# A graph network's second relational layer: neighbour sums in seven half-size block products, and other banks for the root product

## The chip, the cores and the metric

The kernel is one program on one core of a Trainium2 chip. The metric is device time in microseconds, from start to end of one execution; a time without further words is the median of several executions. Everything is in 32-bit floats.

The engines: TensorE (PE in the profile, with its weight loads as PEld) multiplies and writes its sums into PSUM, eight banks of 128 partitions by 512 floats. VectorE (DVE) and ScalarE (ACT) read PSUM and write SBUF. GpSimd (POOL) works on SBUF alone. SyncE (SP) issues most of the transfers. Each engine executes its instructions in the order of the program.

## The reference, cut to what matters

A residual block of attention over a graph of 384 nodes comes first, then a residual block with a two-layer relational graph convolution (768 features, six relations, four basis matrices). The change concerns the latter. Cut down to it:

```python
x = relu(h_text @ w_in + b_in)                       # 384 x 768
for l in range(2):
    h_in = x
    W = einsum('rb,bio->rio', comp[l], basis[l])     # six relations from four bases
    h_all = einsum('ni,rio->rno', x, W)
    msg = h_all[edge_type, src] / counts[edge_type, dst]
    x = segment_sum(msg, dst) + x @ root[l] + conv_bias[l]
    x = relu(x) + h_in
    x = gamma[l] * (x - mean(x, 0)) * rsqrt(var(x, 0) + 1e-5) + beta[l]
h_final = x @ w_out + b_out
return layernorm(h_final) * ln_gamma + ln_beta
```

The kernel turns the gather and the segment sum into dense products. With `H_b = x @ basis_b` for the four bases b, and a 384 x 384 matrix `At_b` for each (edge counts, divided by the degree of the target, mixed over the relations by `comp`), the neighbour sum is the sum over b of `At_b` times `H_b`. It is a product with a contraction of 4 x 384 = 1536.

## The kernel before, in words

The graph's tables are built from the edges in the first half of the kernel, on DVE and POOL, beside the projections of the attention block on PE. At about 388 us (the first L846) the relational layers begin.

Activations lie transposed, as `XT`: features on the partitions, six chunks of 128 (`KC`), by 384 nodes. One layer consists of

- four blocks b, each computing `H[b] = x @ basis_b`, nodes on the partitions (L831 to L872). This product already uses seven half-size products in place of eight. The bank names there are pe, pf, pb, pc and pa, taken by `next_bank` (L70), which hands out the eight banks in a ring, the one longest not taken first. DVE and ACT move and add the results into H (L852 to L867); the last product of a block is left to the next one (`rest`). Between the products DVE mixes the matrices `At` (L326, from `go_between`), and in the first layer the degree counts are computed too: `share` takes a bank `ps_cnt` (L337), and L340 reads it.
- the root product `x @ root` (L880), six output chunks of 128 features, each in a bank `pr[o]`, six matmuls of 384 columns each. `kept` (L835) names the bank that `rest` still needs, so that root's six are taken from the other seven (L877).
- the neighbour sums (`add_neighbours`, L892 to L901), added into the same six banks: for each output chunk o twelve matmuls with a 128x128 piece of H as the weights and 384 columns of `At` moving. All chunks first get bases 0 and 1, then each in turn gets bases 2 and 3.
- the normalisation of chunk o, as soon as its sums are complete (L905 to L918): ACT rectifies with the bias into a buffer `u`, DVE adds the residual into `XN`, measures mean and variance over the 384 nodes (`bn_stats`, `bn_aggr`), adds epsilon, ACT takes the square root, DVE takes the reciprocal, makes scale and offset in three operations on one column, and scales the chunk.

`XN` becomes the next `XT`. After the second layer the output projection (L939) multiplies three tiles of 128 nodes by `w_out`. For the first tile it takes chunks 0 to 3 of `XT` for both halves of the output first, then chunks 4 and 5. DVE normalises the rows and two queues send them out (L943 to L954).

PE, POOL, SP and DVE run in the order of the source (L57), and ACT from L472 on. In the second layer nothing is scheduled in another order than it is written. Waits between engines are derived from what each instruction reads and writes. In tile pools, tiles of one tag share memory: `H` has four buffers, one for a block; `A` holds the tables from which `At` is mixed, and after the last mixing, the rows `rowsB` (L888); `hT` and `mask8` hold the sums of the basis weights (`weight_sums`, L782).

Of the kernel before, what the change touches and what calls it, by code (L numbers as in the profile page):

```python
# [10 lines left out]
F32 = mybir.dt.float32  # L11
# [3 lines left out]
AF = mybir.ActivationFunctionType  # L15
ALU = mybir.AluOpType

P = 128
N = 384
# [32 lines left out]
def gnn_kernel(ctx: ExitStack, tc: tile.TileContext, out, x, edges, chunks, cols, rows, small,  # L52
# [712 lines left out]
    with tc.tile_pool(name="conv", bufs=1) as cp:  # L765
# [60 lines left out]
        T = weight_sums(w)  # L826
        for l in range(L):

            H_ = []
            rest = lambda: None  # L830
            for b in range(B):  # L831
                H_.append(cp.tile([P, NT, DC], F32, tag="H", name="H", bufs=4))
                hs = [[H_[b][:, n, i * HC:(i + 1) * HC] for i in range(2)] for n in range(NT)]
                pe, pf, pb, pc, pa = [next_bank("ps_g")[:, :N] for _ in range(5)]
                kept = ring[-1]  # L835

                def times(ps, x, y, start=False):

                    for c in range(3):
                        nc.tensor.matmul(ps, x[:, c], y(c), start=start and c == 0, stop=(c == 2),  # L840
                                         skip_group_check=not start)

                for c in range(3):
                    for ps, n, i, o, first in ((pa, 0, 0, 0, True), (pe, 2, 0, 0, True), (pf, 2, 0, 1, True),
                                               (pb, 0, 1, 0, True), (pe, 2, 1, 0, False), (pf, 2, 1, 1, False)):
                        nc.tensor.matmul(ps, block(XT, n, i)[:, c], w[c][:, i, o * HC:(o + 1) * HC],  # L846
                                         start=(first and c == 0), stop=(c == 2 and (i == 1 or ps is pa)))
                    if c == 0:
                        rest()
                        T4 = last_sums(w, T[1])  # L850
                    go_between(l, b, c)
                nc.scalar.copy(hs[0][0], pa)  # L852
                nc.vector.tensor_tensor(hs[0][0], hs[0][0], pb, ALU.add)
                times(pc, S[:, 0], lambda c: T[0][:, c], True)
                nc.scalar.copy(hs[2][0], pe)
                nc.scalar.copy(hs[2][1], pf)
                nc.scalar.copy(hs[1][1], pc)
                times(pa, S[:, 1], lambda c: T[1][:, c])
                nc.scalar.copy(hs[0][1], pa)
                times(pc, S[:, 3], lambda c: w[c][:, 1, HC:])  # L860
                nc.vector.tensor_tensor(hs[0][1], hs[0][1], pc, ALU.add)  # L861
                times(pa, S[:, 2], lambda c: T[2][:, c])
                nc.vector.tensor_tensor(hs[1][1], hs[1][1], pa, ALU.add)

                def rest(pa=pa, X=XT, T4=T4, dst=hs[1][0]):
                    times(pa, block(X, 1, 1), lambda c: T4[:, c])
                    nc.scalar.copy(dst, pa)  # L867

                if b + 1 < B:
                    w = load_basis(l, b + 1)  # L870
                    T = weight_sums(w)
                go_between(l, b, 4)  # L872


            w = [wload(root[l, part], "w_c") for part in range(3)]
            XN = xtp.tile([P, KC, N], F32, tag="XT", name="XN")
            pr = [next_bank("ps_c", [i for i in range(8) if i != kept])[:, :N] for _ in range(KC)]  # L877
            for k in range(KC):
                for o in range(KC):
                    nc.tensor.matmul(pr[o], w[k // 2][:, k % 2, o * P:(o + 1) * P], XT[:, k, :], start=(k == 0), stop=False)  # L880
                if k == 0:
                    rest()
                go_between(l, B, k)
            if l + 1 < L:
                w = load_basis(l + 1, 0)
            else:

                rowsB = late.tile([P, 3, D], F32, tag="A", name="rowsB")  # L888
                for j, r in enumerate((R_BOUT, R_LNG, R_LNB)):
                    nc.scalar.dma_start(rowsB[:, j, :], rows[r:r + 1, :].to_broadcast([P, D]))  # L890

            def add_neighbours(o, bs):  # L892
                for b in bs:
                    for n in range(NT):
                        nc.tensor.matmul(pr[o], H_[b][:, n, o * P:(o + 1) * P], At[:, b, n, :],  # L895
                                         start=False, stop=(b == B - 1 and n == NT - 1))

            for o in range(KC):
                add_neighbours(o, (0, 1))
            for o in range(KC):  # L900
                add_neighbours(o, (2, 3))  # L901
                ps = pr[o]
                c = l * KC + o
                u = cp.tile([P, N], F32, tag="u", name="u", bufs=2)
                nc.scalar.activation(u, ps, AF.Relu, bias=cols_sb[:, CB + c:CB + c + 1])  # L905
                nc.vector.tensor_tensor(XN[:, o, :], u, XT[:, o, :], ALU.add)  # L906
                st = tiny.tile([P, 6], F32, tag="stb", name="stb")
                nc.vector.bn_stats(st, XN[:, o, :])
                mv = tiny.tile([P, 2], F32, tag="mvb", name="mvb")
                nc.vector.bn_aggr(mv, st)  # L910
                sc = tiny.tile([P, 3], F32, tag="sc", name="sc")
                nc.vector.tensor_scalar(sc[:, 0:1], mv[:, 1:2], BN_EPS, None, ALU.add)
                nc.scalar.activation(sc[:, 0:1], sc[:, 0:1], AF.Sqrt)
                nc.vector.reciprocal(sc[:, 0:1], sc[:, 0:1])
                nc.vector.tensor_tensor(sc[:, 1:2], sc[:, 0:1], cols_sb[:, GAM + c:GAM + c + 1], ALU.mult)
                nc.vector.tensor_tensor(sc[:, 2:3], mv[:, 0:1], sc[:, 1:2], ALU.mult)
                nc.vector.tensor_tensor(sc[:, 2:3], cols_sb[:, BET + c:BET + c + 1], sc[:, 2:3], ALU.subtract)
                nc.vector.tensor_scalar(XN[:, o, :], XN[:, o, :], sc[:, 1:2], sc[:, 2:3], ALU.mult, ALU.add)  # L918
                if o == 2 and l + 1 < L:
                    T = weight_sums(w)  # L920
# [7 lines left out]
        w = [wload(w_out[part], "w_out") for part in range(3)]  # L928
        for t in range(NT):
            hf = cp.tile([P, NT * DC], F32, tag="H", name="hf", bufs=4)[:, :D]  # L930
            last = t == NT - 1
            ps = [next_bank("ps_f") for _ in range(3 if last else 2)]

            parts = [(ps[0], 0, 512), (ps[1][:, :256], 512, 768), (ps[2][:, :256], 768, D)] if last else \
                [(ps[0], 0, 512), (ps[1], 512, D)]
            for ks in ((range(4), range(4, KC)) if t == 0 else (range(KC),)):
                for p, c0, c1 in parts:
                    for k in ks:
                        nc.tensor.matmul(p, XT[:, k, t * P:(t + 1) * P], w[k // 2][:, k % 2, c0:c1],  # L939
                                         start=(k == 0), stop=(k == KC - 1))  # L940
            st = tiny.tile([P, 4, 6], F32, tag="st", name="st")
            for p, c0, c1 in parts:
                nc.vector.tensor_tensor(hf[:, c0:c1], p, rowsB[:, 0, c0:c1], ALU.add)  # L943
                for c in range(c0, c1, 256):
                    nc.vector.bn_stats(st[:, c // 256, :], hf[:, c:c + 256])
            mv, sd = row_spread(st)

            parts = ((nc.sync, slice(0, 512)), (nc.scalar, slice(512, D)))
            for _, cs in parts:
                nc.vector.scalar_tensor_tensor(hf[:, cs], hf[:, cs], mv[:, 0:1], rowsB[:, 1, cs], ALU.subtract, ALU.mult)  # L950
            nc.vector.reciprocal(sd, sd)
            for queue, cs in parts:
                nc.vector.scalar_tensor_tensor(hf[:, cs], hf[:, cs], sd, x_sb[:, t, cs], ALU.mult, ALU.add)
                queue.dma_start(out[t * P:(t + 1) * P, cs], hf[:, cs])  # L954
# [62 lines left out]
```

## Time and profile before

| what | us |
|---|---|
| median of three runs | 746.15 (744.75 to 747.71) |
| the profiled execution: its time | 747.49 |
| its span | 745.7 |
| PE busy | 724.6 |
| DVE busy | 435.3 |
| ACT busy | 141.8 |
| second layer: root product from 641.29 to 660.64 | 19.35 |
| second layer: neighbour sums from 660.64 to 707.08 | 46.44 |
| in these 46.44 us: DVE busy | 12.79 |
| in these 46.44 us: ACT busy | 3.92 |
| from 707.08 to the end of the span | 38.62 |

Times in the profile are microseconds from the span's start. A line of the timeline gives start, length, engine, source line, operation, what is written from what, and in brackets how long the engine had been idle before and what released it. A matmul in 32-bit floats is one instruction of the source and two records in the trace, each with a weight load. Matmuls are pipelined, so the time from one start to the next, not the duration of one, is what PE spends.

### The profile page before, as it was taken

How to read it: one execution, taken by the hardware profiler on the slowest of the kernel's cores; microseconds unless marked ns; L12 is line 12 of the kernel's file. 1: busy time of each engine (PE TensorE's matmuls, PEld its weight loads, DVE VectorE, ACT ScalarE, POOL GpSimd, SP SyncE). 2: the span in 40 equal slices, each digit the busy share in tenths (PEclk: the TensorE clock that was granted, in tenths of full speed). 3: DMA queues.
4: the chain of work that ended last, by engine and by line, in shares of the span. 5: the costliest groups of instructions: out<-in, count | busy, mean ns of one | idle time of the engine just before them, and what ended most of it. 6: DMA issues, size and time to landing. Idle time of an engine off the chain costs nothing.

```text
span 745.7 us, 7797 instructions
## 1 busy us (share of the span) xinstructions
PE 724.6 (97%) x2820; PEld 471.6 (63%) x2820; DVE 435.3 (58%) x1161; ACT 141.8 (19%) x324; POOL 321.0 (43%) x242
## 2 busy tenths in 40 slices
PE   8999999999999999999899999899999999999995
PEld 7755589999964444446885555555555555555543
DVE  5878518878405499444524699980287766000655
ACT  3301021111102377410121130100022111000200
POOL 1355767778786787587774464210000000210000
PEclk9999999999999999999999999999999999999999
DMA  7797677644356322624428943321003312700001
GB/s 294 254 346 247 190 183 210 202 148 112 114 145 208 57 2 2 212 1 85 86 1 208 277 149 128 127 84 43 0 1 127 113 67 82 289 1 0 0 29 56
DMA packets 40532, 90.94 MB, mean 122 GB/s; under 512 B 19644, under 2 KB 27680, under 8 KB 36270
## 3 DMA queue, kind: packets, MB, share of 16 engines
q1 hardware_dynamic: 18478, 79.62, 30.4%
q0 software_dynamic: 21008, 8.42, 10.3%
q10 hardware_dynamic: 1008, 2.41, 0.8%
q8 instruction: 22, 0.36, 0.2%
q14 instruction: 16, 0.13, 0.0%
HBM read 79.27 MB, written 11.16 MB: 121 GB/s over the span
## 4 chain that ended last, share of the span: by engine, by line
PE 87%; DVE 10%; issue 1%; ACT 1%; DMA 0%; DVEq 0%; ACTq 0%
PE ps_c L895 12%; PE ps_g L846 12%; PE ps_q L395 11%; PE ps_g L840 9%; PE ps_k L377 7%; PE ps_c L880 6%; PE ps_v L525 6%; PE ps_y L616 5%; PE ps_f L939 4%; PE ps_v L377 4%; PE ps_s L564 3%; PE ps_x L377 3%; PE ps_o L609 2%; PE ps_pT L598 2%; DVE same L250 2%; DVE At L326 2%
## 5 line engine op out<-in xcount | busy, mean ns | idle before, releaser
L266 POOL DMA_INDIRECT atab<-count,at x99 | 159.2, 1608 | 55.8 <-DMA atab<-count,at 30.0
L261 POOL DMA_INDIRECT mtab<-m_val,at x99 | 102.3, 1034 | 58.5 <-issue 23.5
L895 PE MATMUL ps_c<-At,H 128*128 128x384 f32 x288 | 93.2, 486 | 0.0
L895 PEld LDWEIGHTS ps_c<-At,H 128*128 128x128 f32 x288 | 54.7, 190 | 38.2
L927 POOL TENSOR_TENSOR x_sb<-x_sb,rowsB 128x1024 f32<-128x1024 f32 x3 | 6.9, 2342 | 159.9 <-DMA rowsB<-in_rows 159.9
L326 DVE SCALAR_TENSOR_TENSOR At<-A,small_sb,At 128x1152 f32<-128x1152 f32 x40 | 62.9, 1635 | 0.0
L840 PE MATMUL ps_g<-T,S 128*128 128x384 f32 x144 | 49.1, 486 | 0.0
L846 PE MATMUL ps_g<-w_c,XT 128*128 128x384 f32 x144 | 48.0, 487 | 0.9 <-DVE H L861 0.9
L846 PE MATMUL ps_g<-w_c,XN 128*128 128x384 f32 x144 | 47.6, 486 | 0.0
L395 PE MATMUL ps_q<-hT,w_q 128*128 128x384 f32 (+1 forms) x160 | 43.4, 436 | 1.4 <-ACT hT L90 1.4
L525 PE MATMUL ps_v<-w_v,v 128*128 128x512 f32 x96 | 41.9, 594 | 0.0
L395 PE MATMUL ps_q<-q,w_q 128*128 128x384 f32 x128 | 41.4, 486 | 0.0
L846 PEld LDWEIGHTS ps_g<-w_c,XT 128*128 128x128 f32 x144 | 27.2, 190 | 20.1 <-DVE H L861 1.5
L846 PEld LDWEIGHTS ps_g<-w_c,XN 128*128 128x128 f32 x144 | 27.4, 190 | 19.1
L840 PEld LDWEIGHTS ps_g<-T,S 128*128 128x128 f32 x144 | 27.4, 190 | 19.1
L395 PEld LDWEIGHTS ps_q<-hT,w_q 128*128 128x128 f32 x160 | 30.2, 200 | 14.1 <-ACT hT L90 1.7
L906 DVE TENSOR_TENSOR XN<-u,XN 128x384 f32<-128x384 f32 x6 | 3.4, 558 | 56.3 <-ACT u L905 56.3
L395 PEld LDWEIGHTS ps_q<-q,w_q 128*128 128x128 f32 x128 | 24.3, 190 | 17.0
L616 PE MATMUL ps_y<-w_o,attT 128*128 128x512 f32 x80 | 35.0, 595 | 0.0
L377 PE MATMUL ps_k<-T,S 128*128 128x192 f32 x192 | 35.0, 326 | 0.0
L342 POOL TENSOR_TENSOR A<-A,rn 128x1152 f32<-128x1152 f32 x6 | 20.1, 3354 | 30.7 <-DVE rn L341 30.7
L577 DVE CUSTOM_DVE_ANT_0 s<-ps_s,mask 128x384 f32<-128x384 f32 x48 | 24.5, 548 | 14.3 <-PE ps_s L564 14.3
(212 smaller groups left out, 1184.2 us busy)
## 6 DMA issues: line engine op xcount, KB each, us to landing
w_c<-in_basis SPq DMA_DIRECT2D x24, 768.0 KB, 6.1
atab<-zero SPq DMA_DIRECT2D x12, 576.0 KB, 7.6
A<-atab POOLq DMA_DIRECT2D x10, 576.0 KB, 10.2
w_c<-in_root SPq DMA_DIRECT2D x6, 768.0 KB, 6.0
w_q<-in_wq SPq DMA_DIRECT2D x4, 1024.0 KB, 11.6
w_q<-in_wiq SPq DMA_DIRECT2D x4, 1024.0 KB, 12.6
w_k<-in_wk SPq DMA_DIRECT2D x4, 1024.0 KB, 5.7
w_k<-in_wik SPq DMA_DIRECT2D x4, 1024.0 KB, 6.2
```

The lines of the kernel that those rows point to most:

```text
L261: nc.gpsimd.indirect_dma_start(mtab[c // PER][:, :], bass.IndirectOffsetOnAxis(at[:, 0, c:c + 1], 0), m_val[:, c:c + 1], None)
L266: nc.gpsimd.indirect_dma_start(atab[0 if i < 18 - DEALT else i % 2][:, :], bass.IndirectOffsetOnAxis(at[:, 1, c:c + 1], 0), count[:, 1, c: ...
L326: nc.vector.scalar_tensor_tensor(At[:, b], A[:, r], w, At[:, b], ALU.mult, ALU.add)
L377: nc.tensor.matmul(ps, a[:, k, :], b[:, k, :], start=start and k == 0, stop=(k == 3), skip_group_check=not start)
L395: nc.tensor.matmul(ps[o][:, c], wt_[:, k, o * P:(o + 1) * P], src[:, k, c], start=(k == 0 and c.start == 0), stop=(k == KD - 1 and c.stop ...
L525: nc.tensor.matmul(ps, v[:, k, t * P:(t + 1) * P], w[k // 4][:, k % 4, :], start=(k == 0), stop=(k == KD - 1))
L616: nc.tensor.matmul(ps, attT[:, k, t * P:(t + 1) * P], w_o[half][k // 4][:, k % 4, :], start=(k == 0), stop=(k == KD - 1))
L840: nc.tensor.matmul(ps, x[:, c], y(c), start=start and c == 0, stop=(c == 2), skip_group_check=not start)
L846: nc.tensor.matmul(ps, block(XT, n, i)[:, c], w[c][:, i, o * HC:(o + 1) * HC], start=(first and c == 0), stop=(c == 2 and (i == 1 or ps is ...
L880: nc.tensor.matmul(pr[o], w[k // 2][:, k % 2, o * P:(o + 1) * P], XT[:, k, :], start=(k == 0), stop=False)
L895: nc.tensor.matmul(pr[o], H_[b][:, n, o * P:(o + 1) * P], At[:, b, n, :], start=False, stop=(b == B - 1 and n == NT - 1))
L939: nc.tensor.matmul(p, XT[:, k, t * P:(t + 1) * P], w[k // 2][:, k % 2, c0:c1], start=(k == 0), stop=(k == KC - 1))
```

## The change

It has three parts.

**The second layer's neighbour sums.** The product is cut in two along each of its dimensions: the output features in pairs of chunks (2p and 2p+1), the nodes in two halves of 192 columns, and the contraction (twelve pieces of 128, four bases by three node tiles) in two groups of six. For every pair seven products of six matmuls with 192 columns replace the eight that these halves would need; some operands are sums of blocks. The sums of `At` (T1 to T4) are made once, ahead of the loop; those of H (`feature_sums`, four a pair) a pair ahead. The results of a product serve several quarters of the output. So only the first products of the three pairs are added into root's banks; ACT then moves each `pr[o]` with its bias into `XN` (`begin`, no rectifier), and DVE adds the rest from two further banks, `pa` and `pc`, while these are still being accumulated (`take`). A rectifier pass on ACT (`rectify`) follows when a chunk is complete. The normalisation is split into `measure` and `normalise_layer`, with reads of the banks (and sums of H) between the two. T3 and one sum of H for each pair are written in place.

**Tiles.** The four H tiles become one; `u` is gone, and in the first layer ACT writes the rectified chunk into `XN`, to which DVE adds the residual in place. `rowsB` becomes the first part of a larger tile `room` in the same memory, whose rest, with `hT` and `mask8`, holds the sums. The output rows `hf` become three parts of one tile in the place of H.

**Root's banks.** In both layers root's six banks now leave out the last two of the ring when a block's banks are taken, `pc` and `pa`, where they left out `pa`.

The diff, cut to its core:

```diff
@@ for l in range(L), blocks of H
-            H_ = []
+            H_ = cp.tile([P, B, NT, DC], F32, tag="H", name="H")
...
-                kept = ring[-1]
+                kept = ring[-2:]
...
-            pr = [next_bank("ps_c", [i for i in range(8) if i != kept])[:, :N] for _ in range(KC)]
+            pr = [next_bank("ps_c", [i for i in range(8) if i not in kept])[:, :N] for _ in range(KC)]
...
-                rowsB = late.tile([P, 3, D], F32, tag="A", name="rowsB")
+                room = late.tile([P, R * NT * N], F32, tag="A", name="room")
+                rowsB = room[:, :3 * D].rearrange("p (j d) -> p j d", j=3)
...
+            def measure(o):
+                nc.vector.tensor_tensor(XN[:, o, :], XN[:, o, :], XT[:, o, :], ALU.add)
...
+                nc.scalar.activation(sc[:, 0:1], sc[:, 0:1], AF.Sqrt)
+                return o, mv, sc
+            def normalise_layer(o, mv, sc):
+                c = l * KC + o
                 nc.vector.reciprocal(sc[:, 0:1], sc[:, 0:1])
...
+            def begin(o, func=AF.Identity):
+                c = l * KC + o
+                nc.scalar.activation(XN[:, o, :], pr[o], func, bias=cols_sb[:, CB + c:CB + c + 1])
+            if l + 1 < L:
+                for o in range(KC):
+                    add_neighbours(o, (0, 1))
+                for o in range(KC):
+                    add_neighbours(o, (2, 3))
+                    begin(o, AF.Relu)
+                    normalise_layer(*measure(o))
+                    if o == 2:
+                        T = weight_sums(w)
+            else:
+                def h(o, i):
+                    return H_.rearrange("p b n d -> p (b n) d")[:, i * 6:i * 6 + 6, o * P:(o + 1) * P]
+                def q(i, j):
+                    return At.rearrange("p b n d -> p (b n) d")[:, i * 6:i * 6 + 6, j * HN:(j + 1) * HN]
+                def times(ps, x, y, start=False, stop=True):
+                    for c in range(6):
+                        nc.tensor.matmul(ps, x[:, c], y[:, c], start=start and c == 0, stop=stop and c == 5,
+                                         skip_group_check=True)
...
+                nc.vector.tensor_tensor(T1, q(0, 1), q(0, 0), ALU.subtract)
+                nc.vector.tensor_tensor(T2, q(1, 1), T1, ALU.subtract)
+                T3 = q(0, 1)
+                nc.vector.tensor_tensor(T3, q(1, 1), q(0, 1), ALU.subtract)
+                nc.vector.tensor_tensor(T4, q(1, 0), T2, ALU.subtract)
...
+                def feature_sums(p):
+                    s0, s1, s3 = spaces[p % 2 * 3:][:3]
+                    o0, o1 = 2 * p, 2 * p + 1
+                    S.append((s0, s1, h(o1, 0), s3))
+                    for dst, x, y, op in ((s0, h(o1, 0), h(o1, 1), ALU.add), (s1, s0, h(o0, 0), ALU.subtract),
+                                          (h(o1, 0), h(o0, 0), h(o1, 0), ALU.subtract),
+                                          (s3, h(o0, 1), s1, ALU.subtract)):
+                        nc.vector.tensor_tensor(dst, x, y, op)
+                        yield
...
+                def take(o, j, ps):
+                    dst = XN[:, o, j * HN:(j + 1) * HN]
+                    nc.vector.tensor_tensor(dst, dst, ps, ALU.add)
+                def rectify(o):
+                    nc.scalar.activation(XN[:, o, :], XN[:, o, :], AF.Relu)
+                    return o
+                def first_of(p):
+                    pa = next_bank("ps_c", range(8))[:, :HN]
+                    times(pa, h(2 * p, 0), q(0, 0), True)
+                    return pa
+                pa = first_of(0)
+                for p in range(pairs):
+                    times(pr[2 * p][:, :HN], h(2 * p, 1), q(1, 0))
+                for o in range(KC):
+                    begin(o)
+                take(0, 0, pa)
+                ready = None
+                for p in range(pairs):
...
+                    pc = next_bank("ps_c")[:, :HN]
+                    times(pc, S[p][0], T1, True)
+                    take(o1, 1, pc)
+                    if ready:
+                        normalise_layer(*ready)
+                    next(sums, None)
+                    times(pa, S[p][1], T2)
+                    take(o0, 1, pa)
+                    next(sums, None)
+                    times(pc, S[p][3], q(1, 1))
+                    take(o0, 1, pc)
+                    ready = measure(rectify(o0))
+                    if last:
+                        pd = next_bank("ps_c")[:, :HN]
+                        times(pd, h(o1, 1), T4, True)
+                        normalise_layer(*ready)
+                        take(o1, 0, pd)
+                        times(pa, S[p][2], T3)
+                        take(o1, 1, pa)
+                        take(o1, 0, pa)
+                        normalise_layer(*measure(rectify(o1)))
+                        continue
+                    times(pa, S[p][2], T3)
+                    take(o1, 1, pa)
+                    normalise_layer(*ready)
+                    for _ in sums:
+                        pass
+                    following = first_of(p + 1)
+                    times(pa, h(o1, 1), T4)
+                    take(o1, 0, pa)
+                    take(o1 + 1, 0, following)
+                    ready = measure(rectify(o1))
+                    pa = following
```

More of the change, by code (lines that the diff above doesn't have):

```diff
@@ L827, in gnn_kernel @@
         for l in range(L):
-            H_ = []
+            H_ = cp.tile([P, B, NT, DC], F32, tag="H", name="H")
             rest = lambda: None
             for b in range(B):
-                H_.append(cp.tile([P, NT, DC], F32, tag="H", name="H", bufs=4))
-                hs = [[H_[b][:, n, i * HC:(i + 1) * HC] for i in range(2)] for n in range(NT)]
+                hs = [[H_[:, b, n, i * HC:(i + 1) * HC] for i in range(2)] for n in range(NT)]
                 pe, pf, pb, pc, pa = [next_bank("ps_g")[:, :N] for _ in range(5)]
-                kept = ring[-1]
+                kept = ring[-2:]
                 def times(ps, x, y, start=False):
@@ L876, in gnn_kernel @@
             XN = xtp.tile([P, KC, N], F32, tag="XT", name="XN")
-            pr = [next_bank("ps_c", [i for i in range(8) if i != kept])[:, :N] for _ in range(KC)]
+            pr = [next_bank("ps_c", [i for i in range(8) if i not in kept])[:, :N] for _ in range(KC)]
             for k in range(KC):
                 for o in range(KC):
-                    nc.tensor.matmul(pr[o], w[k // 2][:, k % 2, o * P:(o + 1) * P], XT[:, k, :], start=(k == 0), stop=False)
+                    nc.tensor.matmul(pr[o], w[k // 2][:, k % 2, o * P:(o + 1) * P], XT[:, k, :], start=(k == 0),
+                                     stop=(k == KC - 1 and l == L - 1))
                 if k == 0:
@@ L894, in add_neighbours @@
                     for n in range(NT):
-                        nc.tensor.matmul(pr[o], H_[b][:, n, o * P:(o + 1) * P], At[:, b, n, :],
+                        nc.tensor.matmul(pr[o], H_[:, b, n, o * P:(o + 1) * P], At[:, b, n, :],
                                          start=False, stop=(b == B - 1 and n == NT - 1))
[L898 to L906, printed above, removed]
+            def measure(o):
+                nc.vector.tensor_tensor(XN[:, o, :], XN[:, o, :], XT[:, o, :], ALU.add)
                 st = tiny.tile([P, 6], F32, tag="stb", name="stb")
@@ L918, in gnn_kernel @@
                 nc.vector.tensor_scalar(XN[:, o, :], XN[:, o, :], sc[:, 1:2], sc[:, 2:3], ALU.mult, ALU.add)
-                if o == 2 and l + 1 < L:
-                    T = weight_sums(w)
+            def begin(o, func=AF.Identity):
[19 more added lines that the diff above has]
+                                         skip_group_check=True)
+                room2 = keep.tile([P, KD * N], F32, tag="hT", name="room2")
+                T1, T2 = [room2[:, i * 1152:(i + 1) * 1152].rearrange("p (c d) -> p c d", c=6) for i in range(2)]
+                T4 = keep.tile([P, 6, HN], F32, tag="mask8", name="T4")
+                nc.vector.tensor_tensor(T1, q(0, 1), q(0, 0), ALU.subtract)
[3 more added lines that the diff above has]
+                nc.vector.tensor_tensor(T4, q(1, 0), T2, ALU.subtract)
+                spaces = [room2[:, 2304:]] + [room[:, 3 * D + i * 768:3 * D + (i + 1) * 768] for i in range(5)]
+                spaces = [v.rearrange("p (c o) -> p c o", c=6) for v in spaces]
+                def feature_sums(p):
[7 more added lines that the diff above has]
+                        yield
+                S = []
+                for _ in feature_sums(0):
+                    pass
+                pairs = KC // 2
+                def take(o, j, ps):
[16 more added lines that the diff above has]
+                for p in range(pairs):
+                    last = p == pairs - 1
+                    sums = iter(()) if last else feature_sums(p + 1)
+                    o0, o1 = 2 * p, 2 * p + 1
+                    pc = next_bank("ps_c")[:, :HN]
[24 more added lines that the diff above has]
+                    for _ in sums:
+                        pass
+                    following = first_of(p + 1)
[4 more added lines that the diff above has]
+                    pa = following
@@ L928, in gnn_kernel @@
         w = [wload(w_out[part], "w_out") for part in range(3)]
+        hf_ = cp.tile([P, NT, D], F32, tag="H", name="hf")
         for t in range(NT):
-            hf = cp.tile([P, NT * DC], F32, tag="H", name="hf", bufs=4)[:, :D]
+            hf = hf_[:, t, :]
             last = t == NT - 1
```

## The prediction

> **What bounds the kernel now.** I read the page first, then the chain of waits, then the timeline of the last 125 us, then the timeline of an earlier stage that already works in half-width products.
>
> The page: TensorE (PE) is busy nearly the whole span, and the chain that ended last is mostly PE.
>
> ```profile
> PE 724.6 (97%) x2820; PEld 471.6 (63%) x2820; DVE 435.3 (58%) x1161; ACT 141.8 (19%) x324; POOL 321.0 (43%) x242
> PE 87%; DVE 10%; issue 1%; ACT 1%; DMA 0%; DVEq 0%; ACTq 0%
> ```
>
> The chain in order of time, for the second layer's end: root product, neighbour sums, output projection (start, length, what). PE follows PE with nothing between. So a microsecond of matmul less in the 46.44 us is a microsecond less in the total, if nothing else becomes late.
>
> ```profile
> 641.45 19.35 PE ps_c L880 x60
> 660.80 46.44 PE ps_c L895 x144
> 707.24 30.94 PE ps_f L939 x84
> ```
>
> A matmul of the source leaves two records here, so 72 matmuls of 384 columns are x144, and one record costs 46.44/144 = 0.3225 us of PE's time. (The 486 ns of its group is its latency; the matmuls overlap.)
>
> The timeline of the "v" projection, which is already done in seven half-width products, gives the price of the new shape: 128x128 weights by 192 columns.
>
> ```profile
> 196.30 1.33 PEld L377 LDWEIGHTS ps_v<-hT,w_v 128*128 128x128 f32 x8
> 196.46 1.46 PE L377 MATMUL ps_v<-hT,w_v 128*128 128x192 f32 x8
> ...
> 197.60 1.33 PEld L377 LDWEIGHTS ps_v<-T,S 128*128 128x128 f32 x8
> 197.76 1.46 PE L377 MATMUL ps_v<-T,S 128*128 128x192 f32 x8
> 198.03 0.35 DVE L497 TENSOR_TENSOR v<-v,ps_v 128x192 f32<-128x192 f32 x1 [2.48 <-PE ps_v L377]
> ...
> 198.90 1.33 PEld L377 LDWEIGHTS ps_v<-hT,S 128*128 128x128 f32 x8
> 199.06 1.46 PE L377 MATMUL ps_v<-hT,S 128*128 128x192 f32 x8
> ```
>
> Products of 8 records start 1.30 us apart (196.46, 197.76, 199.06): 0.1625 us a record, half of 0.3225 within 1%. The weight loads keep up, though none is shared. VectorE (DVE) reads a bank 0.27 us after the next product starts (197.76 to 198.03) and needs 0.35 us.
>
> The timeline of one chunk's normalisation in the second layer, before:
>
> ```profile
> 703.47 0.58 ACT L905 ACTIVATE u<-ps_c,cols_sb 128x384 f32<-128x384 f32 x1 [1.46 <-PE ps_c L895]
> 704.08 0.56 DVE L906 TENSOR_TENSOR XN<-u,XN 128x384 f32<-128x384 f32 x1 [0.78 <-ACT u L905]
> 704.67 0.56 DVE L908 BATCH_NORM_STATS2 stb<-XN 128x6 f32<-128x384 f32 x1
> ...
> 705.67 0.20 ACT L913 ACTIVATE sc<-sc 128x1 f32<-128x1 f32 x1 [1.62 <-DVE sc L912]
> 705.91 0.16 DVE L914 RECIPROCAL sc<-sc 128x1 f32<-128x1 f32 x1 [0.27 <-ACT sc L913]
> ...
> 706.69 0.48 DVE L918 TENSOR_SCALAR XN<-XN,sc 128x384 f32<-128x384 f32 x1
> ```
>
> From this: measuring (add, statistics, epsilon) holds DVE for 1.56 us (704.08 to 705.64), the square root goes to ScalarE (ACT) and back in 0.27, the scaling (reciprocal to the end of L918) takes 1.26. DVE is busy only 12.79 of these 46.44 us, by the table of windows.
>
> **What the Trainium skill says.** "TensorE: Matmul & The Clock Gate", section "Back-to-back issue gap", says that the spacing of a stream of load-and-multiply pairs is set by both operations together. The trace agrees that this must be looked at, and settles it: loads of 190 ns each do not hold 192-column matmuls above 162.5 ns. The same page, "What's actually happening", says that PE falls to half its clock after an idle window of about 3.4 us. This trace shows it already near 2.2 us: after PE's wait for L853 at 478.7, six records took 3.80 us. So a stall of 2 us would cost about 2 us more. "PSUM — Partial Sum Buffer", section "The four PSUM rules", allows a synchronised read in the middle of an accumulation, which the new schedule lives on; the "v" stage shows it. "VectorE: DVE Perf Modes", "The perf-mode tier table", gives f32 additions of two tensors one element a cycle, at 0.96 GHz: 384 more elements cost 0.40 us. Rows here: 0.35 for 192, 0.56 for 384, 0.95 for 768, so 1152 elements are an estimated 1.35.
>
> **Part by part.**
>
> *Products.* Removed: 144 records x 0.3225 = 46.44 us. Added: per pair of output chunks seven products of 6 matmuls, 12 records, 12 x 0.1625 = 1.95 us; 21 products are 40.95 us. If PE never waits: 5.49 us less.
>
> *Sums ahead.* T1 to T4 on DVE (4 x 1.39 with gaps) follow the last add into H, L863, which ends at 636.2, and end near 641.8. Pair 0's four sums (4 x 0.99) need the copy of L867, which lands at 641.97, and end near 646. DVE is idle there until 688 in the old trace, and PE is in the root product until 660.64. Cost nothing, with 14 us of cover; without the cover it would be 9.5 us. POOL's three adds (L927, from 648.4) come after both, and the row loads that they wait for still leave ACT's queue right after L867's copy.
>
> *The loop.* Take 660.64 as 0 and follow the written order. PE: first product and three into root's banks to 7.80, then six products a pair. The wait that is new: each accumulation into pa or pc must wait until DVE has read that bank. Behind a waiting matmul stands all of PE's queue. DVE per full pair: six reads 6 x 0.39, four sums 4 x 0.99, two measurements 2 x 1.60, two scalings 2 x 1.30: 12.1 us (gaps of 0.04 included), against PE's 6 x 1.95 = 11.7. To this come two waits for ACT's rectifier, each 0.54 (0.36 for 192 elements at L742, plus 192 x 0.83 ns from the 0.58 and 0.42 us of ACT rows with 384 and 192 elements). So DVE is the slightly slower engine and slides behind, but each PE wait is for a read one or two products back, and the last pair has no sums. In order:
>
> Pair 0: bank reads done at 10.4, 12.3, 14.3; measurement 14.85 to 16.4; read 16.8; scaling to 18.1; two sums to 20.1; reads 20.5 and 20.9. PE reaches 19.50 without a wait.
>
> Pair 1: the measurement of chunk 1 ends at 22.6, the first read at 23.0, scaling to 24.3, a sum, the second read at 25.68. PE wants that bank at 25.35: a wait of 0.38. Next reads 27.1 and 29.6 (PE would want it at 29.63: 0.01), the last two reads of the pair at 33.3 and 33.65.
>
> Pair 2: PE wants the bank of the 33.65 read at 33.54 (0.16) and the next at 35.65, read at 35.79 (0.19). No sums now, so DVE catches up. The last product ends at 41.69. Waits in all 0.74.
>
> *End of the stage.* The output projection starts on chunks 0 to 3 with 16 records of 0.43 us (30.94 us hold 84 records, 24 of them half as wide, so 72 full ones), to 48.57. The last two reads, rectifier, measurement, square root and scaling of chunk 5 end at 46.90: covered with 1.7 us to spare. What is late next is nothing new; the tail after the last matmul is unchanged, as are the DMAs out.
>
> *First layer.* Its products stay. H in one tile, the activation straight into XN and the lost buffer u change no order and no waited-for instruction; zero, between -0.1 and +0.3. Root's banks: following the ring through the code, the first layer's six were the banks of pa of block 2, pe, pf, pb, pc of block 3, and the fourth count; now pc goes and the fifth count comes, last. PE's wait there is:
>
> ```profile
> PE ps_c L880 <- DVE H L853: 2.2, 1, 2.2
> PE ps_g L846 <- DVE H L861: 0.9, 1, 0.9
> ```
>
> L853 reads pb, which stays fourth, so the wait to 480.92 stays. The fifth count is read at 481.71 to 482.25 (L340), while PE at its low rate reaches that sixth bank about 483.5. Zero; if PE were fast, 0.1 lost. In the second layer the six banks are the same as before.
>
> *Sum.* 46.44 - 41.69 = 4.75, rounded to 4.7 less. Against the profiled execution (747.49 us, span 745.7, 1.8 outside it) that is 742.8; against the median of the runs, 746.15, it is 741.5, which I give.
>
> *Bounds of what the trace doesn't show.* The sums read H in six runs of 128, each 768 apart; the nearest row, L371 with four runs of 128, took 0.68 for 512, in line with 0.95. Were they 1.2 us, the loop ends at 43.2 (gain 3.25). Measurement at 1.8 and scaling at 1.5 give 43.4; sums at 1.2 and reads at 0.55 together 45.1 (1.35). From the other side nothing beats 40.95. I take the rows' values, since the operations are the same ones.
>
> **The rivals.**
>
> A. PE sets the pace, as worked out: 741.5 (740.0 to 742.5). 66 in 100.
>
> B. The bank reads do: DVE's order with longer sums or hand-overs, gain 1.35 to 3.3: about 743.8. For it: 12.1 against 11.7, with two rectifier waits. Against: the slack of one or two products. 22.
>
> C. Slower. The in-place sum into H (pair p+1's part) counts as touching what the next first product reads, if dependencies go by outer bounds and not by the elements. Then that product waits for DVE's two sums: 4.5 us at 15.6 and 5.2 in the next pair, end at 50.75, +4.3, and with about 2 us of half clock for each near 754; it is slower from some 4.8 us of waiting. Against it stands the timeline of the input projection:
>
> ```profile
> 361.97 0.60 ACT L90 ACTIVATE h2T<-ps_h 128x512 f32<-128x512 f32 x1 [4.76 <-PE ps_h L162]
> 362.10 2.58 PEld L377 LDWEIGHTS ps_x<-h2T,w_x 128*128 128x128 f32 x16
> 362.20 2.77 PE L377 MATMUL ps_x<-h2T,w_x 128*128 128x192 f32 x16
> ```
>
> PE multiplies columns 0 to 191 of h2T's first four chunks while ACT, earlier in the program, is still writing columns 256 to 383 of the same chunks: interleaved pieces are kept apart. 6.
>
> D. The bank change also removes the first layer's stall of 2.20 and its slow records (3.80 - 1.94): 4.1 more, 737.4. Against: L853, above. 6.
>
> **How the numbers follow.** Half a per cent, about what a measurement of this kernel can tell from no change, is 3.7 us: below 742.4 is faster, above 749.9 slower. A lies nearly all below (0.62 of its 0.66), D wholly (0.06), B has 0.04 below and the rest between, C above: faster 0.72, same 0.22, slower 0.06. The range goes from 739.6, below A by the spread of the runs (744.75 to 747.71), to 744.8, which takes in most of B; C and D stay out.
>
> **What would show it.** Half-width products 1.95 us apart and a first output matmul near 702 in the trace (707.08 before). PE's waits for DVE reads under 1 us in all, most in pairs 1 and 2. No wait of the output projection for XN. PE's wait for L853 still 2.2. Wrong if: product starts lie more than 2.2 us apart without a wait, DVE never idles from pair 1 on with PE waiting at each product, or PE stops after a pair's fifth product for a sum.

## The result, and the profile after

| what | before | after |
|---|---|---|
| median, 14 runs each, us | 746.14 (744.6 to 749.68) | 740.85 (738.88 to 743.58) |
| ratio after/before, 95% interval | | 0.9924 (0.9908 to 0.994) |
| profiled execution, its time / span | 747.49 / 745.7 | 741.5 / 739.7 |
| second layer's neighbour sums | 46.44 | 40.95 |
| DVE busy in them | 12.79 | 24.17 |

The medians differ by 5.3 us; the ratio's interval is a gain of 4.5 to 6.9 us. The first engine line of the page after:

```profile
PE 719.2 (97%) x2928; PEld 485.6 (66%) x2928; DVE 455.2 (62%) x1196; ACT 144.8 (20%) x330; POOL 321.2 (43%) x242
```

PE has 5.4 us less to do, in 108 records more (252 for 144); DVE has 20 us more. The chain in order of time, after (start, length, what):

```profile
640.94 19.35 PE ps_c L879 x60
660.29 40.95 PE ps_c L946 x252
701.24 30.94 PE ps_f L1053 x84
```

The same three links as before, with no piece of another engine between them: 252 x 0.1625 = 40.95, so PE did not wait once in the new loop. All of PE's waits for other engines from the relational layers on, after:

```profile
PE ps_c L879 <- DVE H L852: 2.2, 1, 2.2
PE ps_g L845 <- DVE H L860: 0.3, 1, 0.3
```

Both stand in the first layer. The first is the old wait at root's fourth bank, unchanged. The second took 0.9 before. The spans differ by 6.0 us: 5.49 in the loop, and 0.5 already there when the loop starts (660.29 for 660.80), about what this second wait differs by.

The timeline after, around the end of pair 0, shows why nothing waited:

```profile
673.78 4.06 PE L946 MATMUL ps_c<-At,H 128*128 128x192 f32 x24
...
674.98 0.56 DVE L901 TENSOR_TENSOR XN<-XN 128x384 f32<-128x384 f32 x1 [0.65 <-ACT XN L981]
...
676.38 0.15 DVE L907 TENSOR_SCALAR sc<-mvb 128x1 f32<-128x1 f32 x1
676.46 0.34 DVE L978 TENSOR_TENSOR XN<-XN,ps_c 128x192 f32<-128x192 f32 x1
...
676.81 0.16 DVE L913 RECIPROCAL sc<-sc 128x1 f32<-128x1 f32 x1
...
677.68 2.11 PE L946 MATMUL ps_c<-T,H 128*128 128x192 f32 x12
677.99 0.95 DVE L968 TENSOR_TENSOR H<-H 128x768 f32<-128x768 f32 x1
678.86 0.95 DVE L968 TENSOR_TENSOR room<-H,room 128x768 f32<-128x768 f32 x1
679.63 4.06 PE L946 MATMUL ps_c<-room,room 128*128 128x192 f32 x24
679.83 0.62 DVE L978 TENSOR_TENSOR XN<-XN,ps_c 128x192 f32<-128x192 f32 x2
...
684.70 0.35 DVE L978 TENSOR_TENSOR XN<-XN,ps_c 128x192 f32<-128x192 f32 x1
```

Three readings. A DVE operation that does not use the result of the one ahead of it starts before that one ends: the bank read at 676.46 starts inside the operation of 676.38, the sum at 678.86 starts 0.87 us after a sum that lasts 0.95, and two reads together take 0.62, not 0.70. Second, the read at 676.46 fills the time of the square root on ACT. Third, PE goes from product to product in steps of 1.95 us, and each read ends before PE wants its bank again: the one at 676.46 ends at 676.80, and the product that adds into its bank starts at 677.68. The tightest read of the loop is that of pair 1's second product, at 684.70: it ends at 685.05, and PE wants the bank at 685.48, 0.43 us later.

### The profile page after: what moved, and what is told of

Its sections match the earlier page's. It is cut to its first block, busy times and chain, and to the rows that moved or that the text cites. A ratio compares the mean times of both kernels' runs of the same rounds, so it can differ in the third digit from the quotient of the medians.

```text
span 739.7 us, 8056 instructions
## 1 busy us (share of the span) xinstructions
PE 719.2 (97%) x2928; PEld 485.6 (66%) x2928; DVE 455.2 (62%) x1196; ACT 144.8 (20%) x330; POOL 321.2 (43%) x242
## 4 chain that ended last, share of the span: by engine, by line
PE 86%; DVE 11%; issue 2%; ACT 1%; DMA 1%; DVEq 0%; ACTq 0%
PE ps_q L395 11%; PE ps_g L845 11%; PE ps_g L839 9%; PE ps_k L377 7%; PE ps_c L896 6%; PE ps_c L879 6%; PE ps_v L525 6%; PE ps_c L946 6%; PE ps_y L616 5%; PE ps_f L1053 4%; PE ps_v L377 4%; PE ps_s L564 3%; PE ps_x L377 3%; PE ps_o L609 2%; PE ps_pT L598 2%; DVE same L250 2%
## 5 line engine op out<-in xcount | busy, mean ns | idle before, releaser
L1040 POOL TENSOR_TENSOR x_sb<-x_sb,room 128x1024 f32<-128x1024 f32 x3 | 6.9, 2342 | 159.8 <-DMA room<-in_rows 159.8
L896 PE MATMUL ps_c<-At,H 128*128 128x384 f32 x144 | 46.6, 486 | 0.0
L896 PEld LDWEIGHTS ps_c<-At,H 128*128 128x128 f32 x144 | 27.4, 190 | 19.0
L525 PEld LDWEIGHTS ps_v<-w_v,v 128*128 128x128 f32 x96 | 18.1, 190 | 22.6 <-issue 22.6
```

The costliest lines, as they stand in the source:

```text
L525: nc.tensor.matmul(ps, v[:, k, t * P:(t + 1) * P], w[k // 4][:, k % 4, :], start=(k == 0), stop=(k == KD - 1))
L896: nc.tensor.matmul(pr[o], H_[:, b, n, o * P:(o + 1) * P], At[:, b, n, :], start=False, stop=(b == B - 1 and n == NT - 1))
```

## The experiments

Each batch ran on one chip beside the kernel before; a ratio is to those runs. L is the length of the second layer's loop in the trace.

| run | median us | ratio, 95% interval | L, us |
|---|---|---|---|
| all but the products | 746.29 | 1.0 (0.9981 to 1.002) | 46.44 |
| old banks | 739.59 | 0.9908 (0.9884 to 0.9931) | 40.95 |
| scaling at once | 743.74 | 0.9967 (0.9952 to 0.9982) | 44.21 |
| half-wide, no block products | 750.55 | 1.0013 (0.9988 to 1.0038) | 46.80 |
| one sum more | 741.24 | 0.9933 (0.9912 to 0.9954) | 42.15 |
| sums twice | 752.54 | 1.0028 (1.0 to 1.0056) | 46.53 |
| sums thrice | 757.47 | 1.0118 (1.008 to 1.0157) | 55.79 |
| both layers | 734.97 | 0.9859 (0.9831 to 0.9888) | 40.95 |
| both layers, again | 734.75 | 0.9842 (0.9812 to 0.9872) | 40.95 |
| and a mixing later | 737.37 | 0.9821 (0.977 to 0.9871) | 40.95 |
| the same, again | 731.89 | 0.9809 (0.9783 to 0.9835) | 40.95 |
| and two mixings later | 731.33 | 0.9804 (0.9777 to 0.983) | 40.95 |

The chip of "half-wide", "sums twice", "sums thrice" and the first "and a mixing later" was the slower one: the kernel before took 749.52 there.

### Which part carries the gain

Everything but the products:

```diff
...
-            if l + 1 < L:
+            if True:
                 for o in range(KC):
                     add_neighbours(o, (0, 1))
...
```

> Everything of the change but the second layer's seven products: one tile for H, no buffer u, rows in the larger tile, root's banks without pc. Theory (the gain is the products' alone): as before, 746.1 within 0.4%; the neighbour sums take 46.4 us again and PE's wait for the add of pb in the first layer is still 2.2 us. Rival (the tiles or banks carry part of the gain, as the 0.6 us that the profile shows ahead of the second layer could suggest): 0.5 to 4 us below 746.1, with a shorter wait in the first layer.

Measured 746.29, ratio 1.0. The wait for the add of pb was 2.2 us, the sums took 46.44. Tiles and banks bring nothing that can be seen; the interval leaves room for 1.5 us either way.

The old banks:

```diff
-                kept = ring[-2:]
+                kept = ring[-1:]
```

> The changed kernel with root's banks as they were (only the last bank left out). Theory: as the changed kernel, 740.9 within 0.4%, since the wait in the first layer is for pb, which is taken either way. Rival (the bank choice matters): slower than the changed kernel by 0.5 us or more, with a longer wait of PE for DVE between 473 and 485 us.

Measured 739.59; the interval overlaps that of the changed kernel, the loop is the same 40.95, the wait again 2.2. The banks are not needed for the gain. The second wait, for L860, was nil in this profile and 1.8 us in that of the run before, in code that is the same in all of these kernels: so the 0.5 us ahead of the loop look like scatter of this kind, not an effect of the change.

Half-wide matmuls alone, in the kernel before:

```diff
...
-                        nc.tensor.matmul(pr[o], H_[b][:, n, o * P:(o + 1) * P], At[:, b, n, :],
-                                         start=False, stop=(b == B - 1 and n == NT - 1))
+                        for j in range(2 if l == L - 1 else 1):
+                            js = slice(j * HN, (j + 1) * HN) if l == L - 1 else slice(0, N)
+                            nc.tensor.matmul(pr[o][:, js], H_[b][:, n, o * P:(o + 1) * P], At[:, b, n, js],
...
```

> The kernel before with the second layer's neighbour sums in half-wide matmuls (each of the 72 split in two of 192 columns, each with its own weight load), and no block products. Theory (price is by columns: 288 records of 0.1625 us are 46.8 against 46.44 us): 0.4 us more, no difference that can be seen. Rival (twice the weight loads cost time, and the block products gained in spite of it): over 50 us for the sums, 750 or more.

The chain of that run:

```profile
659.07 46.80 PE ps_c L897 x288
```

46.80, as expected, and no difference in the time (ratio 1.0013; the median of 750.55 belongs to the slower chip). So the change pays 0.36 us for narrow matmuls and saves one product in eight of 46.80, 5.85.

### How much room DVE has

Scaling at once:

```diff
...
-                    ready = measure(rectify(o0))
+                    normalise_layer(*measure(rectify(o0)))
...
-                    ready = measure(rectify(o1))
+                    normalise_layer(*measure(rectify(o1)))
```

> The changed kernel with each chunk scaled right after its statistics, so that no bank read stands between the two. Theory (DVE has only one or two products of slack): the square root's way to ScalarE and the scaling, 0.27 + 1.18 us, come ahead of the next read; following the order with the durations of the changed kernel's trace gives four PE waits of 0.5 us, 2.1 us in all: 743.0. Rival (the slack is ample, the split does nothing): as the changed kernel, 740.9, no PE wait. Second rival (DVE sets the pace once a read is late): over 4 us slower, above 745.

PE's waits in that run's trace:

```profile
PE ps_c L946 <- DVE XN L978: 2.2, 4, 0.6
```

Four waits, 2.2 us, where 2.1 were expected. The loop, from 659.38 to 703.59 in the chain, took 44.21, 3.26 more than 40.95; each of the four stops costs some 0.26 us besides what the list counts. So putting the reads between statistics and scaling is worth some 3 us of the 5.5. The run moves the scaling (1.18 us) and the square root's way (0.27 us) ahead of the reads together; what each is worth alone was not tried.

More work for DVE; one sum more a pair, then all four twice, then thrice:

```diff
                         nc.vector.tensor_tensor(dst, x, y, op)
+                        if p and dst is s3:
+                            nc.vector.tensor_tensor(dst, x, y, op)
```

> The changed kernel with the fourth sum of H of pairs 1 and 2 issued twice, one DVE operation of 0.97 us more a pair, the output unchanged. Theory (DVE's slack in a full pair is about half a microsecond): following the order again, with the durations of the changed kernel's trace, three PE waits under 0.2 us each, 0.5 us in all, the loop takes 41.5 us. Rival (slack of a whole product, 1.95 us): no wait, 40.95. Second rival (no slack): a wait of about 1 us in each of two pairs, 43.

```diff
+                        again = (s1, s0, h(o0, 0), ALU.subtract) if dst is not s0 and dst is not s1 and dst is not s3 else (dst, x, y, op)
                         nc.vector.tensor_tensor(dst, x, y, op)
+                        for _ in range(1 if p else 0):
+                            nc.vector.tensor_tensor(*again)
```

> The changed kernel with every sum of H of pairs 1 and 2 issued twice (the in-place one followed by a repeat of s1): four more DVE operations of 0.88 us a pair, the output unchanged. Theory (DVE has a slack of about a product, after which every microsecond of it is PE's): following the order with the durations of the changed kernel's trace, PE waits four times, 2.25 us in all, the loop takes 43.2 us and the time is 743.1. Rival (PE's pace has slack enough for 3.5 us more): 740.9, no wait. Second rival (DVE was already full): 7 us more, 748.

> As the run before with every such sum issued three times: eight more DVE operations a pair, 7.0 us. Theory: DVE decides throughout, waits of 7.5 us in all, the loop takes 48.5 us, the time is 748.4, slower than the kernel before the change: of the second doubling nearly all is paid. Rival (slack): below 744.

For thrice, the 1 in `range(1 if p else 0)` is a 2.

With one more sum the loop took 42.15: 1.2 us of waits for 1.94 us of DVE work. That lies between the theory (0.5) and no slack (2): the room of DVE in the loop is some 0.7 us. With the sums twice the loop grew by 5.58, with thrice by 14.84, far above the expected 2.25 and 7.5; the first is nearer to the second rival's 7 than to the theory. Part of the miss lies in the expectation: the sum behind those two numbers left out the repeat of each pair's last sum. Followed again with four repeats it gives 4.0 and 11.1. A repeat that writes what its twin wrote also stood 0.98 to 0.99 us behind it, not 0.88; with the mean spacing of 0.93 in the one run and 0.95 in the other it gives 4.8 and 12.7. Both estimates were made after the runs. The rest, 0.8 and 2.1 us, was not taken apart. In the run with sums thrice a slower clock is part of it. Two of the windows of the run with sums thrice (window, length, busy time of PE, PEld, DVE, ACT, POOL, granted clock of PE as a share of full speed, DMA):

```profile
675.00:685.00 10.00, 8.58 (x53) 8.26 (x52) 8.96 (x19) 0.72 (x2) 0.00 (x0) 1.00 0.00 0
685.00:695.00 10.00, 6.67 (x30) 6.37 (x29) 9.22 (x19) 0.73 (x2) 0.00 (x0) 0.76 0.00 0
```

The clock falls in the second. Its timeline:

```profile
691.12 4.21 PE L946 MATMUL ps_c<-room,room 128*128 128x192 f32 x12 [3.33 <-DVE XN L981]
695.12 3.03 PE L946 MATMUL ps_c<-At,room 128*128 128x192 f32 x12
697.98 4.06 PE L946 MATMUL ps_c<-At,H 128*128 128x192 f32 x24
```

After a stop of 3.5 us the next two products took 4.00 and 2.86 us in place of 1.95 each. The loop has two such stops, with slow records behind them that cost 4.6 us. Without the slow records PE would have waited for DVE in part of that time, so the 4.6 are not all added. Its two stops of 1.4 and 1.6 us, and all those of the run with sums twice, were followed by products at full pace.

### A version that beats both

The first layer's sums in seven products too. The sums of H use three spaces in place of six, since each is read by PE before its successor is written; the next layer's weight sums come after the loop:

```diff
-            if l + 1 < L:
-                for o in range(KC):
-                    add_neighbours(o, (0, 1))
...
-            else:
...
+            room3 = cp.tile([P, 2 * 768], F32, tag="S", name="room3")
+            spaces = [room2[:, 2304:], room3[:, :768], room3[:, 768:]]
...
+            if l + 1 < L:
+                T = weight_sums(w)
             XT = XN
```

> The first layer's neighbour sums in seven block products too; the sums of H in three spaces in place of six, the next layer's weight sums after the loop. Theory (the gain is one product in eight wherever DVE is free in time): the mixing of At ends near 500 us, sums of At near 506 and of H near 509, and the first product that needs one starts near 513, so 5.5 us less again, up to 1 us given back where the weight sums come late: 735 to 736.5. Rival (in the first layer DVE is late with the mixing, so PE waits for the sums): 738 or more, with a PE wait for a sum near 513 or for the weight sums near 558.

> The kernel with both layers in seven products again, the parent for the two runs with moved mixings. Expected: 11.5 us below the kernel before, as in its first run, with the stall of 2.1 us in the first layer.

734.97 and 734.75 on two chips, 11.5 and 10.6 us below the kernel before on the same chip, where the changed kernel was 5.3 below it on its own: 5 to 6 us more. The chain has both loops, without a wait:

```profile
503.15 40.95 PE ps_c L936 x252
...
652.46 40.95 PE ps_c L936 x252
```

The remaining stall in the first layer, which the prediction's rival D had in view, goes with one mixing of At moved behind the adds into H:

```diff
-                   (0, 3, 2): mixes(0, 3, 0, 1), (0, 3, 4): shares(5),
-                   (0, 4, 0): mixes(0, 4, 0, 1), (0, 4, 1): mixes(0, 5, 0, 1), (0, 4, 2): mixes(0, 3, 2, 3),
+                   (0, 3, 4): shares(5),
+                   (0, 4, 0): lambda: (mix(0, 3, At, (0, 1)), mix(0, 4, At, (0, 1))), (0, 4, 1): mixes(0, 5, 0, 1), (0, 4, 2): mixes(0, 3, 2, 3),
```

> Both layers in seven products, and one mixing of the first layer's At (relation 3, bases 0 and 1) moved on DVE from ahead of the last adds into H to behind them, so that the bank that root's fourth chunk takes is read some 5 us earlier. Theory (in the first layer the stall of 2.2 us at root's fourth bank comes from the order on DVE, and the 1.9 us of slow records after it from the stall): 4 us below the kernel with both layers in seven products (734.97): 731. Rival (only the stall goes, the slow records are not its consequence): 732.8. Second rival (DVE's total work decides, the wait turns up later, at the sums of At): no better than 735.

> The kernel with both layers in seven products and relation 3's mixing moved, beside its own parent on one chip. Theory: 4.0 us below the parent. Rival: less than 2 us.

PE's timeline from root's first matmul on, in the kernel with both layers alone:

```profile
473.82 2.10 PE L879 MATMUL ps_c<-XT,w_c 128*128 128x384 f32 x6
477.98 3.89 PE L879 MATMUL ps_c<-XT,w_c 128*128 128x384 f32 x6 [2.06 <-DVE H L852]
481.70 2.10 PE L839 MATMUL ps_g<-T,XT 128*128 128x384 f32 x6
```

and with the mixing later:

```profile
481.13 4.03 PE L879 MATMUL ps_c<-XT,w_c 128*128 128x384 f32 x12
485.00 2.10 PE L839 MATMUL ps_g<-T,XT 128*128 128x384 f32 x6
```

The same work takes 7.88 us (473.82 to 481.70) and 3.87 (481.13 to 485.00): the stall and the slow records after it go together, 4.0 us. The first run of the later mixing, on the slower chip, decides nothing: its interval overlaps that of the kernel with both layers alone. In the medians of one chip the gain was 2.9 (734.75 to 731.89), between the theory's 4 and the rival's 2. The parent's profile there has the stall split in two, 2.0 us at L860 and 0.6 at root's bank. Root then ran at full pace, but the slow records stand behind the other stop:

```profile
453.58 5.83 PE L845 MATMUL ps_g<-w_c,XT 128*128 128x384 f32 x12 [2.03 <-DVE H L860]
```

The next product starts at 459.24, so these twelve took 5.66 us in place of 3.87. So this profile pays some 4.4 us for the stall as well, and why the medians differ by 2.9 alone stays open.

> Both layers in seven products, relation 3's mixing moved as in the run before, and a second mixing of the first layer (relation 1, bases 2 and 3) moved behind the adds into H of block 2 and behind the next block's weight sums. Theory (PE's wait for L860 near 451 us, 0 to 1.8 us from run to run, comes from the adds standing behind that mixing): that wait is gone, up to 1 us below the kernel with the one move. Rival (the mixing is then late for the later ones, and root's banks or the sums of At wait): a new PE wait between 470 and 515 us, same time or slower.

```diff
-(0, 2, 1): mixes(0, 1, 0, 1), (0, 2, 2): mixes(0, 1, 2, 3),
-                   (0, 2, 4): shares(3),
+(0, 2, 1): mixes(0, 1, 0, 1),
+                   (0, 2, 4): lambda: (share(3), mix(0, 1, At, (2, 3))),
```

731.33, and PE waits for no other engine at all from 390 us on; the 0.56 us to the run with one mixing moved are within the scatter. The two profiles with one mixing moved had no wait for L860 either, so that the second move does something is not shown. This is the fastest version, 14 us below the kernel before (731.33 for 745.31 on its chip).

## Why the prediction was right

*Products.* 0.1625 us a record from the "v" stage, 40.95 us for 252: measured to the hundredth. So was the cost of the shape by itself, 46.80.

*Sums ahead.* T4 done near 641.8 and the sums of pair 0 near 646 were forecast; the trace has 640.9 and 645.2, and the sums did run under the root product.

*The loop.* This is the one term that was mis-sized, in the safe direction: 0.74 us of PE waits were forecast, and none came. I had charged every DVE operation its duration and a gap of 0.04, which holds where each uses the result of the last, as in the chunk that I had read from the trace before. In the new order neighbours are mostly independent and overlap: a read takes 0.27 of DVE, not 0.39, a sum 0.88, not 0.99, measurement 1.48, not 1.60, scaling 1.18, not 1.30. A full pair is then 6 x 0.27 + 4 x 0.88 + 2 x 1.48 + 2 x 1.18 = 10.5 us, not 12.1. The two waits for ACT's rectifier come on top, as in the prediction: 0.65 and 0.38 us in the trace where 0.54 each were forecast. That is 11.5, and the trace has 11.85 from pair 0's first measurement (674.98) to pair 1's (686.83), against PE's 11.7. So DVE is about as fast as PE, not faster: it starts with a lead, the last pair has no sums, and the tightest read is 0.43 us early. It is the read for which the prediction had PE wait 0.38. With these durations the same order gives no wait.

*End of the stage.* Chunk 5 was to be scaled 1.7 us before it is needed. It ended at 706.0, and the output projection, started at 701.08, needs it at 707.96: 1.96 us.

*First layer.* Nothing was forecast, and nothing was found: the wait for L853's add stayed 2.2, and the runs without the products and with the old banks agree with their parents within the intervals.

*The sum.* 4.7 us were forecast, 5.3 measured by the medians; with the wait term at its true size it is 5.5. The medians' interval, 4.5 to 6.9, can't tell 4.7 from 5.5; the traces can.

*The rivals.* B, the bank reads set the pace, did not come, but was near: one more sum of 0.97 us a pair brings it on, and scaling at once does too. C, dependencies by outer bounds, did not come: the second half of the 24 records from 673.78, from 675.73 on, is pair 1's first product. It reads H and runs without a stop, while the in-place sum into H that stands ahead of it in the program starts only at 677.99. D's mechanism, that root's banks remove the stall, did not come, for the reason given. Its size was about right: the moved mixing took away 4.0 us in the traces and 2.9 in the medians. Its 3.80 us for six slow records hold the last record's latency; by the starts (480.92 to 484.55) they took 3.63, so 1.7 us are lost, not 1.86.

## What to carry to other kernels

When a PE-bound product is recast into fewer block products, price the narrower shape from a stage that already runs it, and then follow the other engines' order step by step, because the reads between the products are the new limit. Charge dependent operations with their latency and independent ones with their spacing, and count the waits for a third engine too: here they took 1.0 of the 1.6 us that the spacing gave. What makes the reads timely is where they stand in the reading engine's queue: here, putting them ahead of the scaling, into the square root's round trip, was worth more than half of the gain.

## What the runs showed of the hardware

- PE's stops of 2.0 to 2.2 us at root's fourth bank were followed by a stretch at half pace in eight of ten profiles (about five records of 384 columns 0.64 us apart in place of 0.32, some 1.7 us lost), and by full pace in two, those of "all but the products" and "half-wide". Both stops of 3.5 us in the second layer's loop were followed by it, those of up to 1.6 us there never. Length alone doesn't decide: a stop of 2.7 us near 358 us, the same in all fourteen profiles, was followed by it in six.
- The Trainium skill ("TensorE: Matmul & The Clock Gate", section "What's actually happening") speaks of an idle window of about 3.4 us that runs freely. The clock records of the traces agree with such a window, but less than a whole idle one was enough. The granted clock changes only at whole multiples of 3.41 us from its first record in a profile, and a stretch at half clock lasts one window (3.41 us), twice two (6.83). Up to the last matmul, 23 windows at full clock had PE idle for 1.96 us or more, and each was followed by one at half clock; those with 1.94 us or less never were. So a stop costs clock when enough of it falls into one window. Two windows of the changed kernel, then three of "all but the products", whose stop of 2.2 us at the same bank is cut by a border at 478.2 (window, length, busy time of PE, PEld, DVE, ACT, POOL, granted clock, DMA):

```profile
477.30:480.70 3.40, 1.21 (x4) 0.49 (x3) 3.40 (x4) 0.00 (x0) 1.28 (x1) 1.00 0.69 284
480.70:484.10 3.40, 3.40 (x7) 1.83 (x6) 3.37 (x4) 0.00 (x0) 0.00 (x0) 0.50 0.00 0
...
474.80:478.20 3.40, 3.05 (x10) 1.51 (x8) 3.40 (x2) 0.00 (x0) 3.40 (x1) 1.00 1.02 389
478.20:481.60 3.40, 1.54 (x5) 0.83 (x6) 3.37 (x6) 0.00 (x0) 0.12 (x1) 1.00 0.36 148
481.60:485.00 3.40, 3.40 (x12) 2.05 (x12) 3.40 (x2) 0.48 (x1) 0.87 (x1) 1.00 0.00 0
```

- Independent f32 operations on DVE start 0.08 us before the one ahead ends; one that uses the result of the one ahead, or writes what it wrote, starts 0.03 after it (0.99 us apart in place of 0.87).
- Weight loads of 190 ns keep up with matmuls 162.5 ns apart: PEld was busy for the whole 40.95 us and held nothing up.
